# A two-layer graph kernel: the gather of each inner Strassen result is split in two, and one product changes its PSUM bank

## The chip, the core and the metric

The kernel runs on one core of one Trainium2 chip. The metric is the time of one execution on the device in microseconds (us), and the median of three runs is taken. A profile of one further execution shows what each engine did: PE is TensorE (matmuls), DVE is VectorE, ACT is ScalarE, POOL is GpSimd, and SP issues most of the loads.

## The reference, cut to what matters

```python
# layer 0: N = 3327 rows, D = 512
h = relu(layernorm(x))
q, k, v = h @ Wq.T + bq, h @ Wk.T + bk, h @ Wv.T + bv
x = x + softmax(q @ k.T / sqrt(512) + adj + adj, axis=-1) @ v
# layer 1
h = relu(layernorm(x))
A2 = adj + eye(N)
A_norm = d[:, None] * A2 * d[None, :]          # d = diagonal(A2) ** -0.5
x = x + relu(A_norm @ (A2 @ h @ W.T))
```

Everything is float32. Three products with an N x N matrix on one side carry most of the work after the scores: exp(scores) with h, A2 with h, and A2 with the scaled result of that. They are the three **stages** g = 0, 1, 2 of the part that the change touches.

## The kernel before: the parts that matter here

Each stage is a Winograd-Strassen product on two levels. On the outer level there are seven products, p5, p1, p6, p7, p2, p3, p4 in this order. Each is done for two column strips s = 0 and 1, in which an inner matmul is 448 or 384 columns wide. One outer product of one strip is called a **pass**: six paired steps (t = 0 to 5) and then one **unpaired step** (t is None) for the thirteenth row tile. In a paired step an inner Strassen product takes seven matmuls, each into its own PSUM bank, and the banks accumulate over the six steps.

```python
ROLE = {"p1": 0, "p6": 2, "p7": 4, "p5": 6, "p2": 7, "p3": 1, "p4": 5, "p8": 3}

def multiply(self, ps):                      # one step on TensorE
    a, b, w = self.a, self.right.b, Q[self.s]        # w = 448 or 384
    if self.t is None:                               # line 764
        for k, (y, z) in enumerate(((0, 0), (0, 1), (1, 0), (1, 1))):
            yield nc.tensor.matmul(ps[("p2", "p3", "p4", "p8")[k]][:, :w], b[:, z], a[:, 0, y],
                                   start=k == 3, stop=True)
        return
    o = self.o
    for r, i, m in (
        ("p1", 0, a[:, 0, 0]), ("p6", 5, o[:, 2]), ("p7", 6, o[:, 0]), ("p5", 4, o[:, 1]),
        ("p2", 2, a[:, 1, 0]), ("p3", 3, o[:, 3]), ("p4", 7, a[:, 1, 1]),
    ):                                               # line 772
        yield nc.tensor.matmul(ps[r][:, :w], b[:, i], m, start=self.t == 0, ...)

def four_sums(o, g):                         # lines 170 to 172, the o of a later step
    nc.vector.tensor_add(o[:, 0:2], g[:, 0:4:3], g[:, 1:2].to_broadcast([P, 2, g.shape[-1]]))
    nc.vector.tensor_add(o[:, 2], o[:, 1], g[:, 0])
    nc.vector.tensor_add(o[:, 3], o[:, 2], g[:, 2])

def gather(ct, r, s, ps, last):              # after the unpaired step
    ...
    nc.scalar.copy(c11, p["p1"])             # 796
    nc.vector.tensor_sub(c22, p["p6"], c11)  # 797
    nc.vector.tensor_add(c21, c22, p["p7"])  # 798
    nc.vector.tensor_sub(c12, c22, p["p5"])  # 799
    nc.vector.tensor_sub(c22, c21, p["p5"])  # 800
    if into is None:
        nc.vector.tensor_add(c11, c11, p["p2"])   # 802
        nc.vector.tensor_sub(c12, p["p3"], c12)   # 803
        nc.vector.tensor_add(c21, c21, p["p4"])   # 804
        nc.vector.tensor_add(c22, c22, p["p8"])   # 805
    else:                                    # the very last pass: 809 to 812, then 815 x4
        ...
    def settle():                            # the outer level
        for k in range(2):
            if r == "p6":
                nc.vector.tensor_sub(r12[k], to[k], r11[k])
            elif r == "p7":                  # 822, 823, 824
                nc.vector.tensor_add(r21[k], to[k], r12[k])
                nc.vector.tensor_sub(r12[k], r22[k], r12[k])
                nc.vector.tensor_sub(r22[k], r21[k], r22[k])
            elif not place and into is None: # 827, passes p2, p3, p4
                ...
    return settle

def run(k):                                  # one step; each engine works in this order
    ... # the loads for step k + 3; a diagonal correction on DVE in some (line 696)
    if step.t == 0:
        banks_of.update(seven())             # p1 p6 p7 p5 p2 p3 p4
    if step.t is None:
        banks_of["p8"] = bank(ROLE["p8"], "p8")
    for j, _ in enumerate(step.multiply(banks_of)):
        for what, args in within.get(k, ()) if j == 3 else ():
            what(*args)
    rest = gather(...) if step.t is None else None
    steps[k + 2].sums()                      # four_sums for the step after the next
    if rest:
        rest()                               # settle
    for what, args in between.get(k, ()):
        what(*args)                          # right-hand operands, jobs, rows
```

In `between` and `within` stands other work that is spread over the steps. `Right.make` (lines 734 to 740 with 176 to 179) prepares a right-hand operand, and a job (line 851) prepares sums for the later stages. Near the end of stages 0 and 1, `attend` and `temp` multiply finished rows by the weights (line 860 on TensorE, in bank 3; line 872 on DVE or 888 on ACT reads that bank). Near the end of stage 2, `finish` transposes finished rows (line 913, in bank 3; lines 915 and 916 follow). After the last step, six more `finish` calls use banks 0, 2, 4, 6, 7 and 1. Bank 3 is thus shared: p8 of the unpaired step, `attend`, `temp` and `finish` all use it. [...]

## Time and profile before

| | |
|---|---|
| median of 3 runs | 2236.4 us (2235.24 to 2238.02) |
| span of the profiled execution | 2231.7 us |
| PE busy | 2185.5 us, 98% |
| DVE busy | 1623.9 us, 73% |
| ACT busy | 230.7 us, 10% |
| POOL busy | 354.8 us, 16% |

Matmuls are pipelined, and the profile models their ends. A float32 matmul of the kernel appears as two PE instructions. An "idle" figure in brackets is the idle time of the engine just before the instruction, with the instruction that ended it. TensorE's matmuls belong to four lines: 449 (scores, before about 650 us), 772 (paired steps), 764 (unpaired steps) and 860 (rows by weights).

### The profile page before, as it was taken

Reading aid. Unit: us, or ns where it says so; the run is one execution under the profiler, and the core shown is the slowest. Engines: PE = TensorE matmul, PEld = TensorE weight load, DVE = VectorE, ACT = ScalarE, POOL = GpSimd, SP = SyncE. Lnnn points to the kernel's source line nnn. Section 1 sums busy time; section 2 is a strip of 40 time slices with the busy share of each in tenths; the row PEclk is TensorE's granted clock in tenths of the full one; section 3 lists DMA queues with packets and bytes.
Section 4 is the critical chain, followed back from the end, with each engine's and each line's share of the span. In section 5 each row is a group of like instructions: output and inputs, shape, how many; then the busy total and the mean of one; then the engine's idle time right before and its main releaser. Section 6 shows DMA issues by size and latency. Waiting matters only on the chain. (4 is left out here: it accounts for less than half of the span.)

```text
span 2231.7 us, 21005 instructions
## 1 busy us (share of the span) xinstructions
PE 2185.5 (98%) x6268; PEld 1169.3 (52%) x6268; DVE 1623.9 (73%) x3092; ACT 230.7 (10%) x336; POOL 354.8 (16%) x551
## 2 busy tenths in 40 slices
PE   9999999999999999999999999999999999999997
PEld 5555555455545555555444555555544555555554
DVE  6369888788878788877777778886543547777676
ACT  5321121112110000000010000000000000000011
POOL 4223333333321000001221110000000000000001
PEclk9999999999999999999999999999999999999998
DMA  7568888888969998888787899876645458765695
GB/s 253 204 210 309 294 296 287 302 283 305 350 215 329 327 366 283 280 300 272 258 293 240 298 337 355 280 280 202 217 126 195 141 174 299 243 187 185 210 307 172
DMA packets 246682, 583.68 MB, mean 262 GB/s; under 512 B 34768, under 2 KB 106270, under 8 KB 246558
## 3 DMA queue, kind: packets, MB, share of 16 engines
q1 hardware_dynamic: 192270, 399.28, 54.2%
q0 software_dynamic: 44928, 167.49, 19.7%
q10 hardware_dynamic: 9360, 15.47, 2.2%
q8 instruction: 52, 0.85, 0.2%
q14 instruction: 72, 0.59, 0.1%
HBM read 414.28 MB, written 167.85 MB: 261 GB/s over the span
## 5 line engine op out<-in xcount | busy, mean ns | idle before, releaser
L772 PE MATMUL p<-part,b 128*128 128x448 f32 (+1 forms) x3528 | 1255.5, 514 | 5.2 <-DVE part L171 4.9
L772 PEld LDWEIGHTS p<-part,b 128*128 128x128 f32 x3528 | 669.2, 191 | 570.6 <-issue 302.5
L170 DVE TENSOR_TENSOR part<-part 128x896 f32<-128x896 f32 (+1 forms) x252 | 257.0, 1020 | 84.1 <-PE p L772 38.6
L449 PE MATMUL Y<-qt,hp 128*128 128x448 f32 (+1 forms) x832 | 309.2, 514 | 3.9 <-DVE g L453 2.7
L449 PEld LDWEIGHTS Y<-qt,hp 128*128 128x128 f32 x832 | 157.3, 190 | 139.5 <-issue 72.2
L449 PE MATMUL Z<-qt,hp 128*128 128x384 f32 (+1 forms) x416 | 162.6, 513 | 0.0
L172 DVE TENSOR_TENSOR part<-part,part 128x448 f32<-128x448 f32 (+1 forms) x219 | 129.5, 591 | 17.0 <-PE p L772 0.9
L171 DVE TENSOR_TENSOR part<-part,part 128x448 f32<-128x448 f32 (+1 forms) x219 | 129.5, 591 | 7.4
L860 PE MATMUL p<-w,ct 128*128 128x512 f32 x272 | 125.5, 601 | 5.8 <-DVE part L872 4.2
L764 PE MATMUL p<-part,b 128*128 128x448 f32 (+1 forms) x336 | 124.2, 513 | 0.0
L449 PEld LDWEIGHTS Z<-qt,hp 128*128 128x128 f32 x416 | 78.9, 190 | 67.3 <-issue 36.2
L453 DVE SCALAR_TENSOR_TENSOR g<-g,Y 128x384 f32<-128x384 f32 (+1 forms) x156 | 91.6, 587 | 26.9 <-PE Y L449 24.4
L854 POOL DMA_DIRECT2D sum<-job x52 | 28.4, 547 | 488.4 <-DVE job L851 272.9
L797 DVE TENSOR_TENSOR part<-p,part 128x384 f32<-128x384 f32 (+1 forms) x33 | 19.3, 586 | 106.0 <-ACT part L796 57.7
L764 PEld LDWEIGHTS p<-part,b 128*128 128x128 f32 x336 | 63.7, 190 | 53.9 <-issue 33.2
L860 PEld LDWEIGHTS p<-w,ct 128*128 128x128 f32 x272 | 51.9, 192 | 67.7 <-issue 51.9
L796 ACT COPY part<-p 128x384 f32<-128x384 f32 (+1 forms) x33 | 16.5, 499 | 669.1 <-PE p L772 669.1
L449 PE MATMUL X<-qt,hp 128*128 128x384 f32 (+1 forms) x208 | 81.1, 513 | 0.0
L456 ACT ACTIVATE g<-g 128x768 f32<-128x768 f32 (+1 forms) x48 | 43.0, 896 | 352.8 <-DVE g L453 291.8
L860 PE MATMUL p<-w,part 128*128 128x512 f32 x144 | 67.6, 606 | 7.2 <-DVE ct L805 4.8
L441 POOL DMA_DIRECT2D sum<-o x52 | 36.8, 708 | 220.5 <-DVE o L435 156.1
L872 DVE SCALAR_TENSOR_TENSOR part<-p,rs,part 128x512 f32<-128x512 f32 x26 | 19.5, 750 | 64.7 <-PE p L860 56.5
(165 smaller groups left out, 1875.8 us busy)
## 6 DMA issues: line engine op xcount, KB each, us to landing
part<-sum SPq DMA_DIRECT2D x104, 448.0 KB, 5.0
part<-p SPq DMA_DIRECT2D x91, 448.0 KB, 6.4
part<-sum SPq DMA_DIRECT2D x104, 384.0 KB, 3.5
part<-p SPq DMA_DIRECT2D x91, 384.0 KB, 4.1
part<-in_adjT_dram SPq DMA_DIRECT2D x78, 448.0 KB, 4.7
b<-row SPq DMA_DIRECT2D x234, 128.0 KB, 4.9
part<-in_adjT_dram SPq DMA_DIRECT2D x78, 384.0 KB, 3.8
g<-in_adjT_dram SPq DMA_DIRECT2D x52, 448.0 KB, 4.6
```

Source lines behind the costliest of these rows:

```text
L170: nc.vector.tensor_add(o[:, 0:2], g[:, 0:4:3], g[:, 1:2].to_broadcast([P, 2, g.shape[-1]]))
L171: nc.vector.tensor_add(o[:, 2], o[:, 1], g[:, 0])
L172: nc.vector.tensor_add(o[:, 3], o[:, 2], g[:, 2])
L441: nc.gpsimd.dma_start(self.to(sumd)[:, 0:2], self.o)
L449: nc.tensor.matmul(ps[:, :wd], h_of(self.t, name, k), qt[B[name]][:, k], start=start and k == 0, stop=k == 1, skip_group_check=True)
L453: nc.vector.scalar_tensor_tensor(a[n], a[n], 2.0, ps[:, :wd], op0=ALU.mult, op1=ALU.add if sign > 0 else ALU.subtract)
L456: nc.scalar.activation(g[1], g[1], AF.Exp, **({"bias": pad} if self.t == HALF - 1 else {}))
L764: yield nc.tensor.matmul(ps[("p2", "p3", "p4", "p8")[k]][:, :w], b[:, z], a[:, 0, y], start=k == 3, stop=True)
L772: yield nc.tensor.matmul(ps[r][:, :w], b[:, i], m, start=self.t == 0, stop=self.t == PAIRS - 1 and r in ("p1", "p5", "p6", "p7"))
L854: nc.gpsimd.dma_start(sumd[self.s][self.j][:, 2 + self.k], self.a)
L860: nc.tensor.matmul(ps, cts[s][y][d][:, k * P : (k + 1) * P], w[d], start=d == 0, stop=d == DC - 1)
L872: nc.vector.scalar_tensor_tensor(xt, ps, rs[:, i : i + 1], xt, op0=ALU.mult, op1=ALU.add)
```

## The change

The gather is cut in two. Its **first part** (lines 796 to 800 of the kernel before) reads only p1, p6, p7 and p5, which the last paired step finishes. It is now written one step earlier, right after the four sums in step t = 5. Its **rest** (802 to 805), which needs the products of the unpaired step, stays there, but now stands behind the four sums of that step. The fourth product of the unpaired step, p8, leaves bank 3 and goes to bank 0, the bank of p1, which the ACT copy at the head of the first part empties. Since bank 0 now holds p8 until the end of the gather, the first step of the next pass (t = 0) does p1 last. In the very last pass the first part, with its four additions to the outer result, stands in the middle of step t = 5. The change is meant to free the banks of p6, p7 and p5 sooner, to let DVE do the sums while the unpaired step runs, and to leave bank 3 to the row work alone. The arithmetic is the same.

```diff
     def seven():
-        return {r: bank(ROLE[r], r) for r in ("p1", "p6", "p7", "p5", "p2", "p3", "p4")}
+        return {r: bank(ROLE[r], r) for r in ("p6", "p7", "p5", "p2", "p3", "p4", "p1")}
 ... (Step.multiply, paired steps)
-            for r, i, m in (
-                ("p1", 0, a[:, 0, 0]), ("p6", 5, o[:, 2]), ("p7", 6, o[:, 0]), ("p5", 4, o[:, 1]),
-                ("p2", 2, a[:, 1, 0]), ("p3", 3, o[:, 3]), ("p4", 7, a[:, 1, 1]),
-            ):
+            o, first = self.o, [("p1", 0, a[:, 0, 0])]
+            seven = [("p6", 5, o[:, 2]), ("p7", 6, o[:, 0]), ("p5", 4, o[:, 1]),
+                     ("p2", 2, a[:, 1, 0]), ("p3", 3, o[:, 3]), ("p4", 7, a[:, 1, 1])]
+            for r, i, m in seven + first if self.t == 0 else first + seven:
 ... (gather becomes class Gather: first() has lines 796 to 800, rest() lines 802 to 805)
+        def first(self, ps):
+            nc.scalar.copy(c11, p["p1"])
+            nc.vector.tensor_sub(c22, p["p6"], c11)
+            nc.vector.tensor_add(c21, c22, p["p7"])
+            nc.vector.tensor_sub(c12, c22, p["p5"])
+            nc.vector.tensor_sub(c22, c21, p["p5"])
+            if self.last:
+                ... # the four additions of 809 to 812
+        def rest(self, ps):
+            if self.last:
+                ... # the four of 815
+                return
+            nc.vector.tensor_add(c11, c11, p["p2"])
+            nc.vector.tensor_sub(c12, p["p3"], c12)
+            nc.vector.tensor_add(c21, c21, p["p4"])
+            nc.vector.tensor_add(c22, c22, p["p8"])
 ... (run)
-            banks_of["p8"] = bank(ROLE["p8"], "p8")
+            banks_of["p8"] = bank(ROLE["p1"], "p8")
         for j, _ in enumerate(step.multiply(banks_of)):
+            if j == 3 and t == PAIRS - 1 and gatherer.last:
+                gatherer.first(banks_of)
             for what, args in within.get(k, ()) if j == 3 else ():
                 what(*args)
-        rest = gather(cts[step.s], step.r, step.s, banks_of, k == len(steps) - 1) if step.t is None else None
-        if k + 2 < len(steps):
-            steps[k + 2].sums()
-        if rest:
-            rest()
+        sums()
+        if t == PAIRS - 1 and not gatherer.last:
+            gatherer.first(banks_of)
+        if t is None:
+            gatherer.rest(banks_of)
+            gatherer.settle()
         for what, args in between.get(k, ()):
             what(*args)
```

## The prediction, made before any run of the changed kernel

> **What bounds the kernel now.** I read the page first, then the list of waits of PE, then the timeline around each wait. The page says that TensorE is the bound:

> ```profile
> PE 2185.5 (98%) x6268; PEld 1169.3 (52%) x6268; DVE 1623.9 (73%) x3092; ACT 230.7 (10%) x336; POOL 354.8 (16%) x551
> ...
> L772 PE MATMUL p<-part,b 128*128 128x448 f32 (+1 forms) x3528 | 1255.5, 514 | 5.2 <-DVE part L171 4.9
> ```

> The change removes no matmul, so it can only win or lose PE's waits. All of them in the list of PE's waits that lie in the part touched are few and short (the columns are us in total, times, longest):

> ```profile
> PE p L772 <- DVE part L171: 4.9, 4, 1.9
> PE p L860 <- DVE ct L805: 4.8, 2, 4.0
> PE p L860 <- DVE part L872: 4.2, 3, 2.5
> PE pt L913 <- DVE part L824: 3.1, 2, 2.5
> ...
> PE p L860 <- DVE part L827: 2.5, 2, 1.8
> ...
> PE pt L913 <- DVE part L815: 1.6, 1, 1.6
> ```

> With 1.7 us of line 860 after ACT's line 888, these are 22.8 us. The starts of the matmuls tell more than the modelled ends. In an undisturbed stretch the starts of line 772 are 0.376 us apart at 448 columns and 0.3225 us at 384 (the timeline's 14 instructions of a step from start to start), line 860's 0.43 us. I count as **excess** what a start is later than that. After 638 us the excess is 38 us, the ceiling of any gain here: the waits, plus about 0.27 us per wait that the modelled ends hide, plus spells in which spacing doubles. Those spells last 3.4 us and cost 1.5 to 1.8 us each. They follow the excesses 2.10 us (at 883), 2.64 (1064), 4.21 (1215) and 0.72 + 2.69 (2013 to 2016), but not those of 1.94 (1171) or less. So a wait over about 2 us costs some 1.7 us more.

> [...]

> **The change part by part.** DVE's pieces, from the timelines, at 384 / 448 columns: first part 2.26 / 2.5 us, four sums 2.05 / 2.32 us, one operation of the rest 0.47 / 0.53 us from start to start, settle of p7 6 us, of p2 to p4 about 1.8 us. No piece is added; only the order is new.

> *Bank 3 is freed.* In the timeline at 1205 us, line 860 stands behind the unpaired step and needs bank 3, which p8 holds until line 805 has read it:

> ```profile
> 1208.01 3.17 PE L764 MATMUL p<-part,b 128*128 128x448 f32 x8
> ...
> 1209.97 0.51 ACT L796 COPY ct<-p 128x448 f32<-128x448 f32 x1
> ...
> 1214.56 0.61 DVE L805 TENSOR_TENSOR ct<-ct,p 128x448 f32<-128x448 f32 x1
> ...
> 1215.23 3.41 PE L860 MATMUL p<-w,part 128*128 128x512 f32 x4 [4.05 <-DVE ct L805]
> ```

> After the change bank 3 is empty then, and the wait goes: excess 4.21 + 1.5 of slow spell = **5.7 us**. The same at 1762 (0.71 idle) is **1.0**.

> *The sums run while DVE waited.* In 26 of the 41 passes with the plain rest, DVE idles 1.1 to 1.7 us ahead of line 802, for the first unpaired product. The sums (2.05 to 2.32 us) now fill this hole, so the rest ends at about the old time and settle begins 1.5 to 2.0 us sooner. This matters in p7, whose settle delays the sums that PE waits for (line 171). Gone are the excesses at 883 (2.10 + 1.8 spell, **3.8**), 1441 (**1.3**), 1473 (**1.1**) and 1987 (**1.3**). At 2013 to 2016 the transposes wait for settle itself: 1.55 of 3.41 us go, the remaining 1.86 is just under what brought a spell, so I add 0.6 x 1.75: **2.6**.

> *The copy no longer queues.* In stage 1 the ACT copy stood behind line 888; ahead of it, the first part runs during step 5. At 1722 the wait for line 827 goes: **1.0**.

> *At 1044 to 1064,* DVE is some 7 us behind PE, and line 860 at 1064 waits 2.47 us (excess 2.64 + 1.8 spell). The first part moves into DVE's 1.27 us hole ahead of line 872, so DVE is 1 us earlier at the load that this wait hangs on. But p2's bank comes free later: DVE would go first part to 1044.05, operands and bias to 1045.9, line 872 and its norm to 1048.4, sums to 1050.7, line 802 to 1051.3, while PE wants p2 at 1049.56. That 1.9 us wait moves PE toward DVE and removes the later one with its spell; the net is **2.3** with a small chance of a new spell counted.

> *The end.* The four additions of 809 to 812 leave the tail. The last line 815 would end near 2216.3 instead of 2218.2; but the first `finish` uses bank 0, now p8's, and waits for the last addition. Start 2216.35 instead of 2216.98: **0.65**.

> Gains: 5.7 + 1.0 + 3.8 + 1.3 + 1.1 + 1.3 + 2.6 + 1.0 + 2.3 + 0.65 = 20.7 us.

> *What it costs.* Where DVE is behind, the sums now stand ahead of the rest and hold p2's bank. PE asks for p2 as the fourth product of t = 0, 1.94 or 2.26 us after its start. In this timeline (pass p3 of stage 2) DVE has no hole:

> ```profile
> 2141.27 0.69 DVE L740 TENSOR_TENSOR b<-b,rows 128x512 f32<-128x512 f32 x1
> ...
> 2143.03 0.69 DVE L916 TENSOR_TENSOR r<-r,xr 128x512 f32<-128x512 f32 x1
> ...
> 2143.94 5.42 PE L772 MATMUL p<-part,b 128*128 128x448 f32 x14
> ...
> 2145.82 0.55 DVE L802 TENSOR_TENSOR part<-part,p 128x384 f32<-128x384 f32 x1
> ```

> New order: first part 2141.27 to 2143.5, operand 1.76 to 2145.25, line 916 0.6 to 2145.85, sums 2.32 to 2148.2, line 802 to 2148.75. PE wants p2 at 2143.94 + 6 x 0.376 = 2146.2: a **new wait of 2.55 us** and a spell of 1.75, a loss of **4.3**. The same at 1164 (p4 of stage 0): line 802 ends at 1168.85, wanted at 1166.1, 2.75 + 1.75; the wait for 827 that stood at 1171 (1.94 and small change 0.3) shrinks to nothing, so the net loss is **2.3**. At 1261 and 2184 the waits are 1.0 and 0.75, net **0.8** and **0.9** with the small waits that were there. Elsewhere p2's bank is free 0 to 3 us ahead of need, and the operands of the early sums have landed before the unpaired step or within 0.1 us of its start, so the sums won't block on a load. Losses: 8.3 us.

> Net: 20.7 - 8.3 = 12.4 us, so 2236.4 - 12.4 = **2224.0 us**.

> **Rivals.** (1) *The new p2 wait wins.* If the sums ahead of the rest cost a bank wait in more passes than the four found, or if every one brings a slow spell (the waits at 1050, 1261 and 2184 too: 3 x 1.75), the gain falls to some 7 us or less. For: 14 passes have no hole at all ahead of line 802. Against: in nine of them the first part moves into a wait that DVE had earlier, for ACT or for line 860. Time 2229 to 2237. (2) *The holes fill completely and the new waits stay small*, because PE's delay at one place is made up by a wait removed later, as at 1064: gain about 18 us, 2218. (3) *Nothing changes*, because these waits are 1% of the span and others take their place: some waits (872 at 1129 and 1149, 888 at 1681 and 1701, 4 us together) stay in any case. Against: the 4.05 us wait has only the bank as its cause. Time 2236. (4) *p1's bank becomes the new wait,* since p8 is read last. PE asks for p1 six products after the start of t = 0, 3.9 to 4.5 us, while the rest takes only 1.9 to 2.1 us after p2's release: not binding.

> **Range and chances.** The gains have clear causes, the losses depend on where DVE stands to within 1 us, and each spell is worth 1.7 us; three or four doubtful spells and the losses give some 7 us to either side: 2217 to 2232. Two per cent is 45 us, above the whole excess of 38, so faster by over 2% is all but excluded, and a loss of that size would need new waits that no timeline shows.

> **What would show it.** Right: line 860's wait for the last operation of the rest is gone from PE's waits; PE's wait for line 171 falls from 4.9 us to under 1; no DVE hole of 1.4 us or more ahead of the first operation of the rest; new PE waits of line 772 for that operation near 1050, 1166 and 2146, each under 3 us; slow spells at about 1166 and 2146 instead of 883, 1064, 1215. Wrong: waits for the rest in many passes, a wait of the p8 matmul for the ACT copy, or sums that wait for loads ahead of the rest.

## The result and the profile after

The changed kernel takes 2222.28 us (median of six runs, 2219.39 to 2226.49), against 2235.82 us for the kernel before in the same number of runs. The ratio is 0.9941, with a 95% interval of 0.9927 to 0.9955: 13 us, or 0.6%, are gained, and the prediction said 2224.0.

In the changed kernel the first part of the gather has lines 801 to 804 (ACT's copy is 800), the rest 817 to 820, the two closing sets of the last pass 807 and 814, the settling of p7 828 to 830 and that of p2 to p4 833. The rows by weights are line 864, their readers 876 and 892, and the transposes 917. Two lines of the page, busy time and group of the paired steps:

```profile
PE 2179.9 (98%) x6268; PEld 1167.9 (52%) x6268; DVE 1620.2 (73%) x3092; ACT 231.8 (10%) x336; POOL 357.7 (16%) x551
...
L772 PE MATMUL p<-part,b 128*128 128x448 f32 (+1 forms) x3528 | 1255.4, 514 | 9.5 <-DVE part L817 7.6
```

The matmuls cost what they did (1255.4 us, 514 ns each). Yet the idle time ahead of line 772 has risen from 5.2 to 9.5 us, with a new releaser. What was gained stood elsewhere, in the list of PE's waits (us in total, times, longest):

```profile
PE p L772 <- DVE part L817: 7.6, 5, 2.5
...
PE pt L917 <- DVE part L830: 2.2, 1, 2.2
...
PE p L772 <- DVE ct L817: 1.8, 2, 1.5
PE p L864 <- DVE part L876: 1.7, 2, 0.8
PE p L864 <- ACT ts L892: 1.7, 2, 0.8
PE pt L917 <- DVE part L814: 1.3, 1, 1.3
```

The wait for line 171 is gone, and so are the row matmul's waits for 805 and 827. In their place stand seven waits for line 817, the operation that empties p2's bank. One of the signs named beforehand held only in part: DVE still idles 2.9 and 1.4 us ahead of the rest in two passes (near 1651 and 1796), though PE's wait for the rest follows in neither. From the first matmul of line 772 to the last PE instruction, the changed kernel needs 1568.25 us and the one before 1580.72, which is **12.5 us** less; the prediction's sum was 12.4. The two profiled spans differ only by 7.0 us: the changed kernel's profile came to that first matmul 3.9 us later, in code that the change leaves alone, and 1.6 us more passed from its last PE instruction to the end of the span. In eight profiles, the arrival lies anywhere from 637.9 to 644.1 us, whatever the kernel. The end of the span came 6.8 us after the last store had landed in the kernel before and 7.8 to 7.9 us after it in the seven others, among them one whose end is coded as before. I therefore compare the stretch of steps in the traces.

Taken from the start of each pass's unpaired step in both traces, the change of PE's arrival by place is (times of the kernel before, us):

| place | predicted | measured |
|---|---|---|
| 1215 and 1762, bank 3 | -5.7 and -1.0 | -5.7 and -1.0 |
| 883, 1441, 1473, 1987, p7's settling | -3.8, -1.3, -1.1, -1.3 | -3.8, -1.3, -1.1, -1.3 |
| 2013 to 2016, transposes behind p7 | -2.6 | -2.8 |
| 1722, the copy behind line 888 | -1.0 | -1.0 |
| 1044 to 1064 | -2.3 | -2.9 |
| the end | -0.65 | -1.3 |
| 2146 and 1166, new waits with spells | +4.3 and +2.3 | +4.3 and +2.2 |
| 1261 and 2184, new waits | +0.8 and +0.9 | +0.7 and +0.1 |
| 678, 1331, 1395 | none | +1.8, +0.5, +0.4 |

The end is counted at PE's last instruction. The last store landed only 0.7 us sooner than before, counted from the start of the last unpaired step (11.5 us instead of 12.3).

The largest gain and the largest loss can be read in two stretches of the timeline after. The first answers to the one at 1205 us before:

```profile
1209.05 3.17 PE L764 MATMUL p<-part,b 128*128 128x448 f32 x8
...
1212.05 3.60 PE L864 MATMUL p<-w,part 128*128 128x512 f32 x8
...
1214.99 0.61 DVE L820 TENSOR_TENSOR ct<-ct,p 128x448 f32<-128x448 f32 x1
```

Line 864 follows the eight instructions of the unpaired step at once, 2.9 us ahead of line 820, the last of the rest. Before, it stood 4.05 us waiting for that operation. The second answers to the one at 2141 us:

```profile
2131.32 0.55 DVE L804 TENSOR_TENSOR part<-part,p 128x384 f32<-128x384 f32 x1
...
2135.83 0.62 DVE L172 TENSOR_TENSOR part<-part,part 128x448 f32<-128x448 f32 x1
2136.37 0.55 DVE L817 TENSOR_TENSOR part<-part,p 128x384 f32<-128x384 f32 x1
...
2136.97 4.97 PE L772 MATMUL p<-part,b 128*128 128x448 f32 x8 [2.33 <-DVE part L817]
```

DVE finishes the first part (804), then an operand, row work and the four sums, and only then releases p2 (817), for which PE has stood 2.33 us. The eight instructions of the last line take 4.97 us, where eight of the same width take 3.17 us in the stretch above (line 764): that is the half-rate spell that follows. The view by stretches has PE's granted clock at 0.57 there (start and end, length, busy times with counts of PE, its weight loads, DVE, ACT and POOL, then the clock):

```profile
2137.00:2141.00 4.00, 4.00 (x6) 1.81 (x7) 3.94 (x7) 0.00 (x0) 0.00 (x0) 0.57 0.51 204
```

### The profile page after: what moved, and what is told of

It is laid out like the page before. It is cut to its first block, busy times and chain, and to the rows that moved or that the text cites. A ratio compares the mean times of both kernels' runs of the same rounds, so it can differ in the third digit from the quotient of the medians.

```text
span 2224.7 us, 20949 instructions
## 1 busy us (share of the span) xinstructions
PE 2179.9 (98%) x6268; PEld 1167.9 (52%) x6268; DVE 1620.2 (73%) x3092; ACT 231.8 (10%) x336; POOL 357.7 (16%) x551
## 4 chain that ended last, share of the span: by engine, by line
PE 63%; DVE 4%; DMA 1%; issue 1%; ACT 0%; SPq 0%; POOL 0%; ACTq 0%; DVEq 0%; POOLq 0%
PE p L772 51%; PE p L864 8%; PE p L764 4%; DVE part L170 1%; PE pt L917 0%; DMA rows<-row 0%; DVE part L171 0%; DMA part<-sum 0%; DMA xr<-x1d 0%; DVE part L876 0%; DVE part L172 0%; DVE st L190 0%; DVE part L877 0%; DVE part L801 0%; DVE part L817 0%
## 5 line engine op out<-in xcount | busy, mean ns | idle before, releaser
L772 PE MATMUL p<-part,b 128*128 128x448 f32 (+1 forms) x3528 | 1255.4, 514 | 9.5 <-DVE part L817 7.6
L772 PEld LDWEIGHTS p<-part,b 128*128 128x128 f32 x3528 | 668.5, 190 | 575.6 <-issue 308.1
L171 DVE TENSOR_TENSOR part<-part,part 128x448 f32<-128x448 f32 (+1 forms) x219 | 129.5, 591 | 7.4
L764 PE MATMUL p<-part,b 128*128 128x448 f32 (+1 forms) x336 | 124.2, 513 | 0.0
L764 PEld LDWEIGHTS p<-part,b 128*128 128x128 f32 x336 | 63.6, 190 | 54.0 <-issue 33.4
L89 POOL DMA_DIRECT2D out_dram<-r x30 | 16.2, 542 | 303.0 <-DVE r L920 276.3
```

## The experiments

**The bank alone.** This kernel is the one before with p8 in p1's bank and p1 last in t = 0; the gather stays in one piece.

```diff
-            banks_of["p8"] = bank(ROLE["p8"], "p8")
+            banks_of["p8"] = bank(ROLE["p1"], "p8")
 ... (and p1 last in t = 0, as in the change)
```

> The kernel before, with p8 in p1's bank and p1 last in t = 0, but with the gather in one piece. Theory (order of DVE work makes most of the gain, and p1 last costs part of what the free bank 3 brings, because every other bank is asked for one product sooner): the waits of line 860 for the last operation of the gather at 1215 and 1762 go, worth 6.7 us, and waits of 0.3 to 0.9 us for p6 and p2 in the passes where DVE is behind take back some 3 us; 2232 us (2228 to 2235), and the p7 waits for line 171 (4.9 us) stay. Rival (the two parts add up without touching each other): 2229 us, and no new waits of line 772.

It takes 2231.13 us, ratio 0.9986 (0.9978 to 0.9994), and 3.1 us less in the stretch of steps. From its list of PE's waits:

```profile
PE p L772 <- DVE part L171: 4.9, 4, 1.9
...
PE pt L913 <- DVE part L815: 2.9, 1, 2.9
PE p L772 <- DVE part L797: 2.1, 4, 0.8
...
PE p L764 <- ACT ct L796: 0.8, 1, 0.8
```

The waits for line 805 have vanished, p7's 4.9 us stay, and there are new ones: for p6's bank (797), now asked for first, and for the ACT copy that must empty p1's bank ahead of p8. The rival had no new waits, so it falls. One loss was not foreseen: the first transposes at the end use bank 0 and now wait for the last addition (815, 2.9 us instead of 1.6), which costs 1.5 us. By places, the bank brings 4.7 us at 1215, where the wait for the copy is already taken off, and 1.0 at 1762; the waits for the first part elsewhere take back about 1.8. The rest of the 3.1 us are spells, one fewer at 883 and a longer one near 2009, although the waits there are as before. Freeing bank 3 brings little while the copy and the first part come late.

**The split alone.** This is the changed kernel with p8 back in bank 3 and p1 first in every step.

```diff
-            banks_of["p8"] = bank(ROLE["p1"], "p8")
+            banks_of["p8"] = bank(ROLE["p8"], "p8")
-            for r, i, m in seven + first if self.t == 0 else first + seven:
+            for r, i, m in first + seven:
 ... (and p1 first again in the list of seven())
```

> The changed kernel with p8 back in bank 3 and p1 first in every step; only the gather is split and the sums stand ahead of the rest. Theory: p2 is now the fifth product of t = 0, so each new wait for the rest is 0.65 to 0.75 us shorter than in the changed kernel, and the two long ones (near 1167 and 2137) sink below the length that brings a half-rate spell; that gives back about 8 us, while the waits of the row matmul for bank 3 near 1212 (3.6 us and a spell) and 1755 (0.7 us) return, about 7 us: 2222 us (2217 to 2227), the same as the changed kernel. Rival (parts add up): 2229 us, with new waits as long as in the changed kernel.

It takes 2225.34 us, ratio 0.9953 (0.9937 to 0.9968); the stretch of steps is 1569.67 us, 11.0 less than before. Two lines from its list of PE's waits:

```profile
PE p L864 <- DVE ct L820: 4.6, 2, 3.9
...
PE p L772 <- DVE part L817: 3.3, 3, 1.9
```

As the theory has it, the bank 3 wait is back, and the waits for the rest shrink from 9.4 us in seven to 3.3 in three. One detail missed: the wait of 1.9 us near 2142 still brought a spell. The waits trade against each other so closely that the two ratios multiply to 0.9939, the changed kernel's 0.9941. The times alone would pass for two parts that merely add up; only the lists of waits show the trade.

**The rest ahead of the sums.** Here the early first part and the bank stay as in the change, but the sums of the unpaired step follow the rest.

```diff
+        if t is None:
+            gatherer.rest(banks_of)
         sums()
         if t == PAIRS - 1 and not gatherer.last:
             gatherer.first(banks_of)
         if t is None:
-            gatherer.rest(banks_of)
             gatherer.settle()
```

> The changed kernel with the rest of the gather ahead of the four sums of the unpaired step in every pass (the first part stays one step earlier). Theory (the sums ahead of the rest fill DVE's hole in the quiet passes and hold p2's bank in the others): PE's waits for the first operation of the rest (9.4 us in 7) go nearly to nothing, the two half-rate spells at 1168 and 2138 with them, about 14 us; the waits for the third of the sums in the p7 passes (4.9 us with a spell at 883), and longer waits for the settling near 1170 and 2003, return, about 14 us: 2222 us (2216 to 2228). Rival (the sums ahead of the rest are pure gain or do not matter): 2225 us or more with the same waits for the rest, or 2222 with no change in which waits are there.

It takes 2223.08 us, ratio 0.9944 (0.9929 to 0.9958). Two lines from its list of PE's waits:

```profile
PE p L772 <- DVE part L171: 4.9, 4, 1.9
...
PE p L772 <- DVE part L817: 0.2, 1, 0.2
```

The total is that of the changed kernel and the waits change places, as expected. The sums ahead of the rest are what removes p7's 4.9 us, and they are also what makes the new waits for 817. The wait at 883 came back at its old excess (2.09 us, before 2.10), but this time without a spell, which the last section takes up. Partly for that reason, the stretch of steps in this trace is 15.6 us shorter than before, more than the times alone would give.

**Each order where it fits.** In nine of the 42 passes, those where DVE is behind, the rest stands first; elsewhere the sums do.

```diff
+        place = k // len(every)
+        behind = t is None and place in (0, 11, 12, 13, 15, 17, 19, 39, 40)
+        if behind:
+            gatherer.rest(banks_of)
+            if place == 13:
+                gatherer.settle()
         sums()
         if t == PAIRS - 1 and not gatherer.last:
             gatherer.first(banks_of)
-        if t is None:
+        if t is None and not behind:
             gatherer.rest(banks_of)
+        if t is None and place != 13:
             gatherer.settle()
```

> The changed kernel, but in the nine passes where DVE is behind (places 0, 11, 12, 13, 15, 17, 19, 39, 40 of the 42) the rest stands ahead of the four sums, and at place 13 the settling too. Theory: the waits for the rest (9.4 us) and the two spells go, waits of 0.2 to 0.4 us remain at places 13 and 39, and the p7 gains stay: about 14 us less than the changed kernel, 2208 us (2203 to 2214). Rival (DVE is behind there in any order, so the waits only move to the sums or to the row work): 2219 us or more, with new waits of line 772 for line 171 or of the row matmul for the settling.

It takes **2213.01 us**, ratio 0.9896 (0.9879 to 0.9913), and beats both kernels. From its list of PE's waits:

```profile
PE p L864 <- DVE part L876: 3.4, 3, 1.7
...
PE p L772 <- DVE part L817: 0.2, 1, 0.2
```

The stretch of steps is 1557.38 us, 23.3 less than before and 10.9 less than in the change, where 14 were expected. Of some 15 us of waits and spells at the nine places, all but a wait of 0.2 us has gone. Some was given back: at 1064 the row matmul waits again for line 876 (excess 1.8 us), whose row had to be loaded first, since PE now arrives there sooner; the settling wait near 1998 this time brought a spell (1.6); and the end costs 0.3 more. The rival, under which the waits only move, is right for that one place and wrong for the rest.

**p1 first, with p8 in its bank.** This takes the change's odd order out again.

```diff
-            for r, i, m in seven + first if self.t == 0 else first + seven:
+            for r, i, m in first + seven:
 ... (and p1 first again in the list of seven())
```

> The changed kernel with p1 first again in the first step of a pass, while p8 stays in p1's bank. Theory (p1's bank is free only when the last operation of the rest has read p8, and p1 last hides that): PE waits for that last operation at the start of almost every pass, 0.7 to 1.0 us in the some 30 passes where DVE keeps up, 3 to 6 us in the eight or nine where it is behind, those with half-rate spells; together some 60 us, 2280 us (2255 to 2300). Rival (the order of p1 does not matter, p2 is what binds): within 5 us of the changed kernel, waits for the first operation of the rest only.

One run took 2330.23 us (kernel before beside it: 2229.97). Two lines from its list of PE's waits:

```profile
PE p L772 <- DVE part L820: 67.4, 32, 6.2
PE p L772 <- DVE ct L820: 16.7, 8, 3.5
```

In 40 passes, PE waits for line 820, the reader of p8: p1 last is a condition of the bank's move, and worth over 100 us. The time is 30 us above the range given. I had put the single wait in a quiet pass at 0.7 to 1.0 us. Of the 31 waits outside the nine passes where DVE is behind, 15 were 0.6 to 0.7 us, but nine were 1.2 to 1.8 and seven 2.4 to 3.3. In those sixteen passes the rest starts only when the sums end, 2.1 to 4.0 us after the unpaired step began, and not with its first product.

**Waits of chosen length.** Fifteen quiet passes get 9 to 12 more DVE operations ahead of the rest.

```diff
         if t is None:
+            n = {8: 10, 10: 11, 16: 12, 18: 9, ...}.get(k // len(every), 0)
+            for _ in range(n):
+                c = gatherer.parts(gatherer.to)[0]
+                nc.vector.tensor_tensor(c, c, c, op=ALU.max)
             gatherer.rest(banks_of)
```

> The changed kernel with 9 to 12 additional DVE operations (about 0.5 us each, the maximum of a tile with itself, which changes nothing) ahead of the rest in fifteen passes where DVE keeps up. p2's bank is free 2.5 to 3.3 us ahead of need there, so PE should wait 1.5 to 3.1 us for the first operation of the rest in each: some 30 us of waits and a few half-rate spells, 2255 to 2270 us. [...] Rival B (the length of a wait alone decides, at about 2 us): every wait of 2.1 us or more is followed by a spell and none of the shorter ones.

One run took 2316.69 us, more than expected: the operations came 0.66 us apart, not 0.5 (ten in 6.56 us), so the waits grew to 2.9 to 6.4 us. That serves the question all the same. PE's timeline at two of them:

```profile
948.71 4.46 PE L772 MATMUL p<-part,b 128*128 128x384 f32 x13 [3.42 <-DVE part L817]
...
1390.29 5.19 PE L772 MATMUL p<-part,b 128*128 128x384 f32 x10 [2.77 <-DVE part L817]
```

and the stretches behind them (start and end, length, busy times with counts, then PE's granted clock, here 1.00 and 0.51):

```profile
949.00:952.40 3.40, 3.40 (x12) 1.94 (x12) 3.40 (x6) 0.00 (x0) 0.00 (x0) 1.00 0.02 7
...
1390.50:1394.00 3.50, 3.50 (x6) 1.75 (x6) 3.50 (x6) 0.00 (x0) 0.00 (x0) 0.51 0.02 7
```

The longer wait cost no clock (the trace has no half-rate record between 848 and 1021 us) and the shorter one did. Rival B, the length alone, falls with that. The starts of half-rate records have a grid in the traces: in the kernel before they lie at 883.63, 1064.54, 1214.72 and 2016.85 us, which is 53, 44 and 235 times 3.413 us from one to the next, and each record lasts 3.41 us. On the grid of this run's own records, the wait of 3.42 us (excess 3.59) stood 1.73 us in one interval and 1.86 in the next; the excess of the other, 2.93 us, stood wholly in one. A sharp limit is not shown: at 982 a wait left 2.18 us in one interval without a spell, and at 2150 one left 2.07 us in one interval and a spell followed.

## Why the prediction held, and where it was off

The steps of the prediction held in kind and mostly in size, as the table shows: bank 3, p7's settling, the copy and the two long new waits were each within 0.3 us. Ceiling and sign followed from PE being the bound. Two of the matches are partly luck. At 883 the old trace had a spell; the two experiments that kept this wait had none, so 1.7 of the 3.8 us would not be there to win in every run. At 2013 to 2016 the prediction left 1.86 us of wait, and 2.33 us were left. The term came right only because no spell followed; in the mixed order and in the split alone one did, and the same place gained only 1.2 us. Three terms were off.

- *"Elsewhere p2's bank is free 0 to 3 us ahead of need"* failed at three places, 2.7 us together. At 678 (+1.8), the old timeline left next to no room, which was read as enough. Most of this loss is a late load: in the changed kernel's profile DVE's sums for t = 0, which wait for a load there, began 0.6 us ahead of the unpaired step, while in the seven other profiles it was 1.8 to 2.4. The last experiment has the same order of work in this pass, and with the load in time the excess is 0.5 us instead of 1.7. At 1331 and 1395 an operand's preparation, which used to stand ahead of the first part, now stands between it and the sums.
- *1044 to 1064* and *2184* were too gloomy by 0.6 and 0.8 us. These were readings of DVE's place, good to within such amounts. *The end* was put at 0.65 us for the start of the first transposes, which came only 0.3 us sooner; but the twelve instructions then followed each other in 1.5 us, where before they took 2.6 with waits for line 815 between them. Hence the 1.3 us at PE.
- *The threshold of a spell* was put at a wait of about 2 us. The size of a spell was right, but whether one follows did not go by the length alone. It came out right in sum because the two long waits, 2.49 and 2.70 us of excess, each lay in one interval of the grid of 3.413 us on which the half-rate records start (2137.58 and 1168.19 us in this trace), while the 2.33 us of the transposes was split into 0.84 and 1.50 and went free.

Rival 1 (new p2 waits) came true in part: there were waits in more passes than the four, for 2.7 us, but only the two long ones brought spells. Rival 2 (18 us, the new waits stay small) fell with those two, which cost 6.5 us; rival 4 (p1's bank) does not bind only because p1 comes last, which the p1-first run shows. Rival 3 would have had nothing change, and it fell. The split alone shows that p2's bank is asked for 0.7 us sooner because p1 no longer stands ahead of it. The prediction's count of p2 as the fourth product contained this, but it didn't name it as a price of the bank's move.

## What to carry to other kernels

Where one engine is busy 98% of the time, list its waits and lay out, for each, in what order the releasing engine comes to the release. That gave a gain of 12.4 us against 12.5 measured, from the old trace alone, though with two spells of some 1.7 us each that could have fallen the other way. An order that fills a hole in one pass holds a buffer in another, so decide it by pass: the mixed order brought 23.3 us of steps in its trace where the fixed orders brought 12.5 and 15.6, and 21.1 us in the medians where they brought 13.5 and 11.0. When two resources are exchanged, compare the lists of waits and not the totals, for the totals of the two halves can look independent while their waits trade.

## What the runs showed of the hardware

The traces also show how much idle time it took in these steps. In the kernel before, the intervals with 3.41, 2.64 and 2.54 us of idle time were each followed by half rate, and so were those with 2.70 and 2.49 us in the changed kernel; over all eight traces I counted some 40 with 2.2 us or more, and each was. Waits split into 1.73 and 1.86 us (chosen length), 1.00 and 0.94 (before, at 1171) or 0.84 and 1.50 (changed, at 2006) were not. In between both occur: 2.07 us (chosen length, at 2150) and 2.10 us (before, at 883) brought half rate, 2.03 us (the rest ahead of the sums, at 883) and 2.18 us (chosen length, at 982) did not; why is not shown. So the same 2.1 us wait cost 1.7 us of clock at 883 in the kernel before and nothing in the two experiments that kept it, the bank alone, where it was split, and the rest ahead of the sums. At some 1.7 us each, such waits can shift a run by a few us; whether they make the spread that was measured between runs is not shown.

ACT did not take up its copy ahead of work that it had been given earlier: in the kernel before it stood idle for 8.31 us, ran line 879 at 1209.25 us and only then, at 1209.97, the copy (796), although the last product for p1 had started at 1202.75.
